# The setup stores, the early weight loads and the relation sums of a graph-network kernel, put in another order

## The chip, the cores and the metric

The kernel runs on one core of one Trainium2 chip. The metric is device microseconds of one execution; several executions are timed and the median is given. A profile comes from one further execution. The engines are named as the profile names them: PE (TensorE, the matmuls; PEld is its weight load), DVE (VectorE), ACT (ScalarE), POOL (GpSimd) and SP (SyncE, which only starts transfers). PSUM is the memory that matmuls write, SBUF the working memory, DRAM the large one. Each engine works through its own instructions in order, and an instruction that starts a DMA is one of them: what stands behind an instruction that waits, waits too.

## The reference

Eight layers follow each other on a node table `x` of 3125 rows and 256 columns, with 50000 edges (`src`, `dst`, sorted by `dst`); each layer takes the layer norm of `x` and adds its result to `x`. The first four, of which the change touches the first, are cut to what matters here:

```
x = x + rel_graph(ln(x))          # rows of src times one of 16 matrices, by edge type, times a weight, summed by dst
x = x + experts(ln(x))            # 8 experts, 2 per node, gelu
x = x + edge_graph(ln(x))         # embedding rows of src, times edge features @ W_dist, summed by dst, then W_comb
x = x + top_half_mlp(ln(x))
...                               # attention graph, experts, max graph, experts
```

```python
transformed = jnp.einsum('ni,rio->rno', h, weight)
msg = transformed[rel_type, src] * norm
out = jax.ops.segment_sum(msg, dst, num_segments=h.shape[0])
```

## The kernel before

**Setup (lines 366 to 679).** The edges come in as [125 x 400] tiles: `dsti` (destinations) on SP's queue, `srci`, `typi`, `wgt` and `norm` on ScalarE's. `x` is loaded in five groups `n_x0` to `n_x4` of five node tiles of 126 rows each (`xs0`, line 415), all on SP's queue. There is a branch for unsorted destinations (line 459), which these inputs do not take. After it the order of PE, DVE, ACT, POOL and SP is the order of the program (`manual_schedule`, line 538): nothing is moved by a scheduler.

The destinations, as floats (`dstf`), are stored to a DRAM table `dsr` (lines 542 and 543), and to the edge records `md` with the sources, the code of destination and type, the weight and a padding (lines 544 to 599). GpSimd gathers from `dsr` the row in which each node's edges begin (`find.fetch`, tile `q_rows`), VectorE counts in it (`find.count`), a small matmul turns the counts into `mixI`, and GpSimd gathers with it the first node tile's edge records (`meta_load`, tile `m_m`). On the same queue of GpSimd, in program order, stand 25 gathers of embedding rows (`species`, tile `n_row`): 5 ahead of the branch, 3 ahead of the two `q_rows` gathers, 7 behind them, and 10 behind `m_m`. VectorE takes the statistics of `x` (`stats`) for groups 0 and 1, then of group 2 woven with the inverse root of the first ten, then norms; groups 3 and 4 come after `mixI`. Each group of five node tiles is stored to the DRAM table `tab` (line 633), 1.26 MB, when its normed rows and its embedding rows are there.

**The tile loop (`stage_one`, line 787 on).** For each of 25 node tiles come 21 windows of 128 edges (17 in the last), and then eight steps of `weigh`. Each of these 29 steps ends in `between()`, one slot. A window gathers 128 rows of `tab` (tile `g`, GpSimd, nine buffers), loads 65 x 128 edge features (tile `f`, SP, six buffers), multiplies `g` with a selection matrix `s` that VectorE has built two windows ahead (`build`, lines 865 and 867; PE line 880 into the PSUM tile `c`), and the features with `w_d` (line 887 into `pw`), which VectorE multiplies with the embedding half of `g` (tile `mt`, line 890). ScalarE copies `c` to `aT` for two windows at once (line 884; `c` has two PSUM banks). `weigh` multiplies `aT` with the 16 relation matrices `w_rel` into one PSUM bank (also called `f` in the profile, line 919), and after its last step VectorE adds this sum to `x` (line 923).

Every second tile a `Flow` begins, for a pair of tiles: `route`, `experts` and `combine`, cut into steps that `between()` hands out slot by slot, so that they fill the engines beside the windows of later tiles. `between()` also advances `bg` (the later search and edge sums), one load of weights (`late_weights`, on ScalarE's queue: `w_rel` in two halves of 2.1 MB in the first two slots, then 0.26 MB pieces of the experts' weights) and one zero store (`first_zeros`, on SP's queue: 32 pieces of 197 KB of the sum table `ex`, then the experts' token tables). After the last tile the Flows that are left run in rounds with nothing beside them.

The rest of the kernel, from 1865 us on, is not touched.

Of the kernel before, what the change touches and what calls it, by code (L numbers as in the profile page):

```python
# [9 lines left out]
F32 = mybir.dt.float32  # L10
# [11 lines left out]
NT = 25  # L22
# [23 lines left out]
TN = 126  # L46
# [49 lines left out]
def tile_gnn_ffn(ctx: ExitStack, tc: tile.TileContext, a: dict, out: bass.AP):  # L96
    nc = tc.nc
# [14 lines left out]
    def ps(tag, shape):  # L112
        return banks["pool"].tile(shape, F32, name=tag, tag=tag, bufs=banks["bufs"][tag])
# [60 lines left out]
    def flat(v):  # L174
        return v.rearrange("(p t) -> p t", p=EP)
# [131 lines left out]
    dsr = dram.tile([EP + 1, ET], F32, name="dsr")  # L307
# [10 lines left out]
    def split(pool, dsti, pre):  # L318

        hii = pool.tile([EP, ET], I32, name=pre + "hii")  # L320
        hif = pool.tile([EP, ET], F32, name=pre + "hif")
        lof = pool.tile([EP, ET], F32, name=pre + "lof")
        dstf = pool.tile([EP, ET], F32, name=pre + "dstf")
        nc.vector.tensor_scalar(hii, dsti, 7, None, op0=OP.arith_shift_right)
        nc.vector.tensor_copy(hif, hii)
        nc.vector.tensor_copy(dstf, dsti)
        nc.vector.scalar_tensor_tensor(lof, hif, -128.0, dstf, op0=OP.mult, op1=OP.add)
        return hif, lof, dstf
# [68 lines left out]
    def rows126(table, t, n):  # L397
        return table[t * TN : (t + n) * TN, :].rearrange("(t p) d -> p t d", p=TN)

    def edge_in(name, dt):  # L400
        t = pp.tile([EP, ET], dt, name="e_" + name)
        nc.scalar.dma_start(t, flat(a[name]))
        return t
# [1 line left out]
    srci = edge_in("src", I32)  # L405
    typi = edge_in("edge_type_16", I32)
    xs0 = []
    for i in range(5):
        xg = pp.tile([P, 5, D], F32, name=f"n_x{i}")
        t = 5 * i  # L410
        m = 5 if i < 4 else 4
        if i == 4:
            nc.gpsimd.memset(xg[:, 4, :], 0.0)
            nc.sync.dma_start(xg[:TV, 4, :], a["x"][(NT - 1) * TN :, :])
        nc.sync.dma_start(xg[:TN, :m], a["x"][t * TN : (t + m) * TN, :].rearrange("(t p) d -> p t d", p=TN))
        xs0.append(xg)
        if i == 0:
            wgt = edge_in("edge_weight", F32)
            norm = edge_in("edge_weight1", F32)
    nc.scalar.dma_start(wd[0:1, :], a["L1_gnn_b_dist"])  # L420
    nc.scalar.dma_start(wd[1:65, :], a["L1_gnn_W_dist"])
    eid = pp.tile([EP, ET], F32, name="e_eid")
# [1 line left out]
    none = pp.tile([1, ET], F32, name="e_none")  # L424
# [34 lines left out]
    with tc.If(uns > 0):  # L459

        rec = dram.tile([E, RW], F32, name="rec")
        with tc.tile_pool(name="srt", bufs=1) as ep, tc.tile_pool(name="srt2", bufs=2) as eb, \
# [13 lines left out]
            hif, lof, dstf = split(ep, dsti, "s_")  # L476
# [11 lines left out]
            for b in range(ET // BT):  # L488
# [11 lines left out]
                for i in range(BT):  # L500
                    j = b * BT + i
# [37 lines left out]

    dstf = pp.tile([EP, ET], F32, name="e_dstf")  # L540
    nc.vector.tensor_copy(dstf, dsti)
    nc.sync.dma_start(dsr[1:, :], dstf)
    nc.sync.dma_start(dsr[:1, :], none)
    nc.sync.dma_start(flat(md[F_DST, :E]), dstf)
    pf = ps("tp", [P, EP])
    nc.tensor.transpose(pf, dstf[:, 0:1].to_broadcast([EP, P]), ident[:EP, :EP])
# [50 lines left out]
    nc.sync.dma_start(flat(md[F_NORM, :E]), norm)  # L597
    nc.sync.dma_start(flat(md2[F_EID - 5, :E]), eid)
    nc.sync.dma_start(md[:, E:].rearrange("f (p c) -> p f c", c=P), pads)


    lt = pp.tile([EP, ET], F32, name="e_lt")
# [46 lines left out]
    def meta_load(t, pool):  # L649
        m = pool.tile([R1, P], F32, name="m_m", bufs=2)  # L650
        gather(m, words(md), mixI[:R1, t : t + 1])
        return m
# [29 lines left out]
    def late_weights(pool, w):  # L682

        def loads(name, dst, src):
            w[name] = dst
            nc.scalar.dma_start(dst, src)

        def rows(m, name):
            k, n = m.shape
            return pool.tile([P, k // P, n], F32, name="w_" + name), m.rearrange("(k p) n -> p k n", p=P)  # L690

        def same(src, n):
            return bass.AP(tensor=src.tensor, offset=src.offset, ap=[[0, P], [1, n]])

        for k in range(2):
            nc.scalar.dma_start(wrel[:, k], a["L0_gnn_weight"][:, k * P : (k + 1) * P, :].rearrange("r p o -> p r o"))
            yield
        loads("rw0", *rows(a["L0_ffn_router_w"], "rw0"))
        loads("b01", pool.tile([P, 16], F32, name="w_b01"), a["L0_ffn_b1"])
        loads("b02", pool.tile([8, D], F32, name="w_b02"), a["L0_ffn_b2"])  # L700
        yield
        w["01"] = pool.tile([P, 8, 2, 256], F32, name="w_01")
        w["02"] = pool.tile([P, 8, 2, 256], F32, name="w_02")
        for e in range(8):
            nc.scalar.dma_start(w["01"][:, e], a["L0_ffn_w1"][e].rearrange("(k p) f -> p k f", p=P))
            yield
            nc.scalar.dma_start(w["02"][:, e], a["L0_ffn_w2"][e].rearrange("(f p) d -> p f d", p=P))
            yield
        loads("c", *rows(a["L1_gnn_W_comb"], "c"))
        yield  # L710
        nc.scalar.dma_start(wfa[:, :, :D], a["L2_gnn_W_func"].rearrange("(k p) n -> p k n", p=P))
        loads("bc", pool.tile([P, D], F32, name="w_bc"), same(a["L1_gnn_b_comb"], D))
        loads("wr", pool.tile([P, D], F32, name="w_wr"), same(a["L1_ffn_wr"], D))
        yield

    def first_zeros():
        exv = ex.rearrange("(p r) d -> p (r d)", p=TN)
        for c in range(0, NT * 2 * D, ET):
            nc.sync.dma_start(exv[:, c : c + ET], zero[:TN])
            yield  # L720
        nc.sync.dma_start(tab2[NX:, :], zero[: NP - NX, :ZW])
        nc.sync.dma_start(rec2[E:, :], zero[:, :2])
        for f in range(3):
            nc.sync.dma_start(md2[f, E:].rearrange("(p c) -> p c", c=P), zero[:NPAD, :P])
        yield
        for x, y in zip(xg2 + xg3, yg2 + yg3):
            w = y.shape[0] // P * D
            v = x[: y.shape[0], :].rearrange("(p r) d -> p (r d)", p=P)
            for c in range(0, w, ET):
                nc.sync.dma_start(v[:, c : min(w, c + ET)], zero[:, : min(w, c + ET) - c])  # L730
                yield
# [55 lines left out]
    def stage_one(late, cp, eb):  # L787
# [83 lines left out]
        cur = {}  # L871
# [42 lines left out]
        def weigh(t, i):  # L914
            if i == 0:
                cur["f"] = ps("f0", [P, D])
            for r in (2 * i, 2 * i + 1):
                for h in range(2):
                    nc.tensor.matmul(cur["f"][:TN], aT[:, h, r, :], wrel[:, h, r, :], start=(r == 0 and h == 0),  # L919
                                     stop=(r == 15 and h == 1))  # L920
            if i == 7:
                x = x_of[t // 2][:TN, t % 2, :]
                nc.vector.tensor_add(x, x, cur["f"][:TN])


        x_of, e_of = {}, {}

        def size(q):
            return min(2, NT - 2 * q)
# [10 lines left out]
        def load_e(q, i):  # L940
            n = size(q)
            e = e_of[q, i] = eb.tile([P, 2, D], F32, name=f"e{i}", bufs=1)
            nc.sync.dma_start(e[:TN, :n], rows126(ex, 2 * q, n)[:, :, i * D : (i + 1) * D])
# [190 lines left out]
        flows = []  # L1134
        bg = background(eb, bank)
        loads, zeros_ = late_weights(late, w), first_zeros()
        slot = 0

        def between(fast=False):
            nonlocal slot  # L1140
            for i, f in enumerate(flows):
                f.step(slot, flows[:i], fast)
            while flows and flows[0].part == 3:
                flows.pop(0)
            if slot < 2 * PERIOD or slot % BG_EVERY == 0:
                next(bg, None)
            next(loads, None)
            next(zeros_, None)
            slot += 1

        meta(0)
# [7 lines left out]
        for t in range(NT):  # L1159
            n = GL if t == NT - 1 else GC  # L1160
            for j in range(n):
                build()
                window(k)
                k += 1

                if j >= 2:
                    at = wins[k - 2][1]
                    if at in (3, 0):
                        add_up(t, 0 if at == 3 else 1)
                if j == 3 and t + 1 < NT:  # L1170
                    raw[t + 1] = meta_load(t + 1, wb)
                if j == META_AT and t + 1 < NT:
                    meta(t + 1)
                if j == 14 and t % 2 == 0:
                    load_x(t // 2)
                if j == 18 and t == 1:
                    beyond(eb, bank())
                if t % 2 and j == 19:
                    load_e(t // 2, 0)
                between()  # L1180
            for i in range(8):
                weigh(t, i)
                if i == 1:
                    add_up(t, 2)
                if i == 7 and (t % 2 or t == NT - 1):
                    if t == NT - 1:
                        load_e(t // 2, 0)
                    flows.append(Flow(t // 2))
                between()
        while flows:  # L1190
            between(True)
# [1349 lines left out]
```

## Time and profile before

| | |
|---|---|
| Median of 3 runs | 4229.56 us (4227.59 to 4244.47) |
| The profiled execution's own time, and its span | 4229.5 us, 4227.7 us |
| Setup: last `tab` store landed | 84.5 us |
| First `f` matmul of `weigh` in the first tile | 148.7 us |
| Last add of a relation sum | 1762.7 us |
| First load of the next stage | 1865 us |
| Busy over the span: PE, DVE, POOL, ACT | 64%, 46%, 42%, 20% |

Section 2 of the profile page cuts the span into 40 slices of 106 us. The digits are tenths of busy time, PEclk the granted clock in tenths:

```
PE   1688999989889999948411365365670112137875
DVE  3445666665665555442344333444662233245300
POOL 4342333341253333002466544544437666643323
DMA  7766455452243444113233254365523333323543
```

The first slice is the setup and the start of the first tile; the tile loop is slices 2 to 17. A share of busy time says little in itself: the waits and the timeline of a stretch say what ended each stretch of idleness. A wait is written `who <- for whom`, with the time in all, the number of times, and the longest.

### The profile page before, as it was taken

The numbers are of one execution on the slowest core, as the hardware profiler recorded it, in microseconds if no ns is written. First come the engines' busy times: TensorE is split into PE (matmuls) and PEld (weight loads), VectorE is DVE, ScalarE is ACT, GpSimd is POOL, SyncE is SP. The second block draws the span as 40 slices with busy tenths as digits, with TensorE's granted clock in tenths as the row PEclk, the third lists the DMA queues.
The fourth block names the chain that finished last, engine by engine and source line by source line (L and its number), as shares of the span: only waits on it lengthen the run. The fifth ranks groups of instructions, "written<-read, shape, count | busy, mean of one in ns | idle before, by whom it ended". The sixth has DMA issues, their size and how long they took to land. (4 is left out here: it accounts for less than half of the span.)

```text
span 4227.7 us, 46661 instructions
## 1 busy us (share of the span) xinstructions
PE 2697.7 (64%) x12940; PEld 2134.4 (50%) x12940; DVE 1946.6 (46%) x7501; ACT 845.3 (20%) x1803; POOL 1758.5 (42%) x1996
## 2 busy tenths in 40 slices
PE   1688999989889999948411365365670112137875
PEld 0566878767677878737310254254550111125653
DVE  3445666665665555442344333444662233245300
ACT  1112232221122222211100021122220000013322
POOL 4342333341253333002466544544437666643323
PEclk9878999999799999968755576577775555566987
DMA  7766455452243444113233254365523333323543
GB/s 223 223 190 187 129 157 144 130 154 65 76 118 107 118 133 126 52 48 107 73 93 91 86 175 141 107 185 168 174 90 101 87 92 88 92 81 107 158 159 100
DMA packets 275971, 521.46 MB, mean 123 GB/s; under 512 B 53609, under 2 KB 176897, under 8 KB 275685
## 3 DMA queue, kind: packets, MB, share of 16 engines
q0 software_dynamic: 105344, 306.57, 25.0%
q1 hardware_dynamic: 159598, 201.27, 15.6%
q10 hardware_dynamic: 10742, 10.34, 0.8%
q8 instruction: 114, 1.87, 0.2%
q14 instruction: 173, 1.41, 0.1%
HBM read 431.19 MB, written 86.78 MB: 123 GB/s over the span
## 5 line engine op out<-in xcount | busy, mean ns | idle before, releaser
L136 POOL DMA_INDIRECT g<-tab,m_si x521 | 498.0, 956 | 989.9 <-DVE mt L890 526.5
L136 POOL DMA_INDIRECT g_rows<-tab,srcI x413 | 401.9, 973 | 300.4 <-DVE ACC L2273 157.3
L136 POOL DMA_INDIRECT g_row<-tab,srcI x413 | 400.4, 970 | 196.3 <-issue 104.6
L880 PEld LDWEIGHTS c<-s,g 128*128 128x128 f32 x2084 | 345.8, 217 | 166.7 <-issue 83.9
L880 PE MATMUL c<-s,g 128*128 128x96 f32 x2084 | 356.1, 299 | 100.1 <-issue 38.2
L887 PE MATMUL pw<-w_d,f 65*128 65x256 f32 x1042 | 374.4, 445 | 14.2 <-DVE mt L890 11.9
L919 PE MATMUL f<-w_rel,aT 128*126 128x256 f32 x1600 | 372.6, 383 | 0.1
L884 ACT COPY aT<-c 128x384 f32<-128x384 f32 (+1 forms) x323 | 237.1, 737 | 595.7 <-PE c L880 397.5
L1982 PE MATMUL mm<-ro_xt,ro_w 128*128 128x192 f32 (+3 forms) x928 | 255.9, 428 | 122.3 <-ACT ro_h L2063 73.1
L919 PEld LDWEIGHTS f<-w_rel,aT 128*126 128x126 f32 x1600 | 300.2, 190 | 50.5 <-issue 5.3
L1651 PE MATMUL tp<-ident,ACC 128*128 128x128 f32 x50 | 16.1, 424 | 462.5 <-DVE ACC L2395 357.2
L890 DVE TENSOR_TENSOR mt<-pw,g 128x256 f32<-128x256 f32 x521 | 218.7, 420 | 159.0 <-PE pw L887 83.8
L1986 PE MATMUL y<-ro_w,ro_h 128*96 128x256 f32 (+2 forms) x1040 | 263.6, 409 | 33.5 <-ACT ro_h L2063 19.1
L1982 PEld LDWEIGHTS mm<-ro_xt,ro_w 128*128 128x128 f32 x928 | 183.8, 221 | 178.4 <-ACT ro_h L2063 80.5
L1651 PEld LDWEIGHTS tp<-ident,ACC 128*128 128x128 f32 x50 | 7.1, 199 | 470.5 <-issue 441.1
L1986 PEld LDWEIGHTS y<-ro_w,ro_h 128*96 128x96 f32 (+2 forms) x1040 | 190.4, 189 | 86.9 <-ACT ro_h L2063 23.1
L1037 PE MATMUL w<-w,b_h 128*126 128x256 f32 x800 | 218.5, 398 | 11.1 <-ACT xt L950 3.0
L1028 PE MATMUL w<-xt,w 128*128 128x252 f32 (+1 forms) x832 | 221.3, 392 | 6.3 <-issue 3.4
L140 POOL DMA_INDIRECT xg<-XX,ro_pos x100 | 101.6, 1016 | 287.6 <-issue 136.5
L2273 DVE SCALAR_TENSOR_TENSOR ACC<-g_rows,g_e,ACC 128x256 f32<-128x256 f32 x413 | 200.9, 486 | 43.9 <-DVE ACC L2273 19.9
L2395 DVE TENSOR_TENSOR ACC<-ACC,g_row 128x256 f32<-128x256 f32 x413 | 173.2, 424 | 67.1 <-DMA g_row<-tab,srcI 48.0
L2240 PE MATMUL pu<-w_s,a_xt 128*128 128x256 f32 x100 | 45.9, 606 | 231.5 <-DVE ACC L2268 104.8
(580 smaller groups left out, 4791.0 us busy)
## 6 DMA issues: line engine op xcount, KB each, us to landing
ro_w<-in_L_ffn_blocks SPq DMA_DIRECT2D x58, 514.0 KB
ro_w<-in_L_ffn_blocks SPq DMA_DIRECT2D x58, 512.0 KB
f<-in_attr_t SPq DMA_DIRECT2D x521, 32.5 KB
xg<-zero SPq DMA_DIRECT2D x78, 200.0 KB
b_at<-in_edge_attr SPq DMA_DIRECT2D x100, 125.0 KB
tabr<-v SPq DMA_DIRECT2D x12, 758.0 KB
g<-tab,m_si POOLq DMA_INDIRECT x521
g_rows<-in_L_ffn_blocks SPq DMA_DIRECT2D x14, 514.0 KB
```

Source lines behind the costliest of these rows:

```text
L136: return nc.gpsimd.indirect_dma_start(out=dst, out_offset=None, in_=table, in_offset=bass.IndirectOffsetOnAxis(ap=idx, axis=0))
L880: nc.tensor.matmul(pc[:, h, o : o + GW], g[:, h * P : (h + 1) * P], sums[k][0], start=True, stop=True)
L884: nc.scalar.copy(aT[:, :, :, b : b + n * GN].rearrange("p k r n -> p k n r"), pc[:, :, : n * GW].rearrange("p k (n r) -> p k n r", r=16))
L887: nc.tensor.matmul(pw, feats.pop(k), wd, start=True, stop=True)
L890: nc.vector.tensor_tensor(mt[0], pw, rows.pop(k)[:, D:], op=OP.mult)
L919: nc.tensor.matmul(cur["f"][:TN], aT[:, h, r, :], wrel[:, h, r, :], start=(r == 0 and h == 0), stop=(r == 15 and h == 1))
L1028: nc.tensor.matmul(ph, w["01"][:, e, k, i * P : (i + 1) * P], xt[:, k, : n * TN], start=(k == 0), stop=(k == 1))
L1037: nc.tensor.matmul(py, last[:, k, i * TN : (i + 1) * TN], w["02"][:, e - 1, k, :], start=(k == 0), stop=(k == 1))
L1982: nc.tensor.matmul(ph, w[:, o : o + P], xt[:, k, :], start=(k == 0), stop=(k == 1))
L1986: nc.tensor.matmul(py, h[:, i, s], w[:, i * D : (i + 1) * D], start=(i == 0), stop=(i == self.fc - 1))
L2273: stt(u, g[:, r, :D], e[:, r0 + r : r0 + r + 1], u, op0=OP.mult, op1=OP.add)
L2395: nc.vector.tensor_tensor(u, u, rows.pop(r), op=OP.max)
```

## The change

Three places are changed.

1. The stores of `dstf` and of one row of -1 into `dsr` go to ScalarE's queue instead of SP's. The loads of groups 2 to 4 of `x` move on SP's queue from ahead of the branch to behind the stores of the edge records. The memset for the last tile's padding moves with group 4, on GpSimd to behind the seven gathers of embedding rows.
2. In `between()` the weight loads begin in slot 2 and the zero stores in slot 6, instead of both in slot 0.
3. The relation sum of tile t is added to `x` in the second window of tile t + 1 (`weighed`), and the Flow of a pair begins there, two slots later; the last tile's is added at once, as before.

```diff
-    for i in range(5):
+
+    def load_x0(i):
         xg = pp.tile([P, 5, D], F32, name=f"n_x{i}")
...
-        if i == 0:
-            wgt = edge_in("edge_weight", F32)
-            norm = edge_in("edge_weight1", F32)
+
+    load_x0(0)
+    wgt = edge_in("edge_weight", F32)
+    norm = edge_in("edge_weight1", F32)
+    load_x0(1)
...
-    nc.sync.dma_start(dsr[1:, :], dstf)
-    nc.sync.dma_start(dsr[:1, :], none)
+    nc.scalar.dma_start(dsr[1:, :], dstf)
+    nc.scalar.dma_start(dsr[:1, :], none)
...
     nc.sync.dma_start(md[:, E:].rearrange("f (p c) -> p f c", c=P), pads)
+    for i in range(2, 5):
+        load_x0(i)
...
-            if i == 7:
-                x = x_of[t // 2][:TN, t % 2, :]
-                nc.vector.tensor_add(x, x, cur["f"][:TN])
+
+        def weighed(t):
+            x = x_of[t // 2][:TN, t % 2, :]
+            nc.vector.tensor_add(x, x, cur["f"][:TN])
+            if t % 2 or t == NT - 1:
+                flows.append(Flow(t // 2))
...
-            next(loads, None)
-            next(zeros_, None)
+            if slot >= 2:
+                next(loads, None)
+            if slot >= 6:
+                next(zeros_, None)
             slot += 1
...
                 window(k)
                 k += 1
+                if j == 1 and t:
+                    weighed(t - 1)
...
-                if i == 7 and (t % 2 or t == NT - 1):
-                    if t == NT - 1:
-                        load_e(t // 2, 0)
-                    flows.append(Flow(t // 2))
+                if i == 7 and t == NT - 1:
+                    load_e(t // 2, 0)
+                    weighed(t)
```

## The prediction

> **What bounds the kernel now.** I read the slices of the page first, then the waits and the timeline of the first 150 us, then TensorE's waits in the long tile loop. The chain that ended last starts only at 3997 us, so it says nothing of the place that the change touches; I followed that chain by hand.
>
> The waits of GpSimd and VectorE up to 90 us (who waited <- for what: us in all, times, longest):
>
> ```profile
> POOL q_rows L136 <- DMA dsr<-e_dstf: 16.3, 1, 16.3
> ...
> DVE j L798 <- DMA tab<-n_row: 24.4, 1, 24.4
> DVE q_rows L578 <- DMA q_rows<-dsr,q_rowi: 13.0, 2, 12.5
> ```
>
> The reader is to see a stall in the setup: GpSimd does nothing for 16.3 us until the destinations are in DRAM (`dsr`), and VectorE ends the setup with 24.4 us of waiting for `tab`. The timeline shows why (start, us, engine, line, what, count):
>
> ```profile
> 19.45 6.80 SPq L415 DMA_DIRECT2D n_x<-in_x  x1
> 35.23 0.32 SPq L542 DMA_DIRECT2D dsr<-e_dstf  x1
> ...
> 19.57 0.37 DVE L541 CAST e_dstf<-dsti 125x400 f32<-125x400 int32 x1 [6.92 <-DVEq L459]
> ...
> 39.76 0.91 POOL L136 DMA_INDIRECT q_rows<-dsr,q_rowi  x1 [16.33 <-DMA dsr<-e_dstf]
> ...
> 52.21 0.97 POOL L136 DMA_INDIRECT m_m<-md,mixI  x1 [1.21 <-DVE n_st L616]
> ...
> 65.29 1.00 POOL L136 DMA_INDIRECT n_row<-in_L_gnn_embed_table,l_z  x1 [0.30 <-issue]
> ```
>
> `e_dstf` is ready at 19.94, its store leaves SP at 35.23: it stands behind x's loads, each of which waits for the DMA eight before it to land (eight completion semaphores in turn, by the built program). Behind it GpSimd's 17 remaining embedding gathers (1.30 us apart) end at 66.3, the last `tab` store can only then go, and `tab` is complete at 84.5. Nothing of the tile loop starts before. The windows of 5 us show what the DMA engines do (columns: busy us of PE, PEld, DVE, ACT, POOL; clock; DMA share; GB/s):
>
> ```profile
> 30.00:35.00 5.00, 0.00 (x0) 0.00 (x0) 4.36 (x25) 0.50 (x1) 0.00 (x0) 1.00 0.11 32
> 35.00:40.00 5.00, 0.00 (x0) 0.00 (x0) 0.00 (x0) 4.52 (x10) 0.24 (x1) 1.00 0.26 78
> ...
> 70.00:75.00 5.00, 0.00 (x0) 0.00 (x0) 0.00 (x0) 0.00 (x0) 0.00 (x0) 1.00 0.93 350
> ```
>
> They idle during the stall and are full afterwards, to about 150 us (0.93 at 300 GB/s on average over 90 to 148.7). So the first tile, too, is held by transfers. From 407 to 1762 us TensorE is busy 1270 of 1355 us; what it waits for is small:
>
> ```profile
> PE c L880 <- issue: 20.9, 18, 5.3
> PE c L880 <- DVE s L865: 15.6, 13, 3.8
> PE pw L887 <- DVE mt L890: 7.9, 9, 1.4
> ```
>
> **What the Trainium skill says.** "DMA: Bandwidth & Descriptors", Issuing engines are not separate DMA queues: a DMA issued on another engine saves only the issuer's time. The trace agrees as to issue (0.32 us for the store) but here 15 us of waiting stood ahead of it in SP's order, and that is what the move takes away; it brings no bandwidth. Same page, Measured: 1 MB moves at 341 GB/s, 16 MB at 425; the trace's best slice of the setup is 375, so I price a full queue at 350. "TensorE: Matmul & The Clock Gate", What's actually happening: the array runs at half clock until it has been busy for about 3.4 us. The trace has it: four `c` matmuls take 1.01 us at 93.9 and 0.58 at 146.67, though the granted clock reads 1.00 in both; a first tile with fewer gaps may warm sooner. I take nothing for that.
>
> **Part 1: destinations on ScalarE's queue, x2 to x4 behind.** Removed: the wait of 15.3 us (35.23 - 19.94). ScalarE has nothing until its activation at 24.24; the two stores (0.32, 0.21) and the table load (1.28) behind them end by 22, so that costs nothing. From issue to GpSimd's gather took 4.5 us (39.76 - 35.23): the gather can go at 24.5. The two `q_rows` gathers (1.22 apart) and seven embedding gathers (1.30) end at 36.1. Without the cover of that work the gain on GpSimd would be the whole 15.3; but the next gather, `m_m`, needs VectorE's count.
> VectorE: statistics of groups 0 and 1 end at 29.6 as now; group 2 is loaded late. SP issues `srcf` at about 22.6 and is through `pads` 4.4 us later (as 36.25 to 40.66 now), x2 goes at 27.0. It is 0.63 MB behind about 0.8 MB of md stores; at 220 GB/s (what 5 to 20 us show) that lands at about 33. VectorE so stalls 3.5 us, and the norms of groups 0 and 1 move from 34.3 to 38. Then the counts, already landed, follow at once: `mixI` at 41.5 instead of 49.7, `m_m` (2.5 us later, as now) at 44 instead of 52.2, say 9 us earlier with rounding. x4's load waits on SP for a memset that now sits behind the seven gathers on GpSimd (36.4); it lands by about 42 and is used at about 45, so it is hidden; should x3 or x4 be 5 us late, the norms of the last 15 tiles are (50 to 55), still ahead of GpSimd's end. GpSimd's last gather ends at 57.3 (66.3 - 9). The cut stores and two `tab` stores stand behind x4's load on SP, and go at 41 to 44, as now (43.03).
> From GpSimd's end to `tab` complete are 18.2 us now (84.5 - 66.3). In that stretch the first half of `w_rel`, 2.1 MB issued at 58.24, shares the engines: 6 us at 350 GB/s. Part 2 takes it out. `tab` complete: 57.3 + 18.2 - 6 = 69.5, that is 15 us earlier.
>
> **Part 2: weights from slot 2, zeros from slot 6.** The 2.1 MB now load inside the first tile, whose transfers fill the engines: +6 us (7 at the 300 GB/s of that stretch; bound below by 0 if it fits between gathers, above by the 15.6 us that ScalarE stood at 94 to 110, when its in-order queue waited at the DMAs behind the other half and `aT`, the evacuation of `c`, with them). Six zero pieces of 0.197 MB leave the first tile: -4 us at 300 GB/s. They come after slot 115, where the DMA share is 0.62 (250 to 407): hidden, at most +4. The embedding `e` of the first pair is read at slot 48, the last `ex` zero goes at slot 37: no new wait.
>
> **Part 3: the sum added in the next tile.** The same 25 adds of 0.42 us. VectorE waits 133.2 us in 22 of them, 6 each, but TensorE is at work then. Without it VectorE does the last slot's steps and the next selection matrices before the tile ends instead of after: at 463.57 it adds, and the first `s` comes 1.6 us later, while TensorE shows no gap at all. What can be had lies in the 15.6 and 7.9 us quoted; I take a fifth, -5 us over the loop (bounds: 0 and -20, nearly all). Each Flow starts two slots later; the PSUM bank of the sum is free 20 slots before it is needed. At the end Flow 11 is two rounds behind: about 98 rounds from 1763 to 1864, so 1.03 each, +2 us.
>
> **Sum.** -15 + 6 - 4 - 5 + 2 = -16, against the profiled execution's own 4229.5 us (span 4227.7 and 1.8 around it), which is within 0.1 us of the median of the three runs. So 4214.
>
> **Rivals.** *More* (4200): nothing of `w_rel` is paid (it loads while gathers wait on GpSimd's 1.25 us each), and every boundary gives 0.6 us: -15 - 4 - 13 + 2 = -30. For it: first-tile gaps of 4 to 6 us that are latency, not bytes. Against: the DMA share is 1.0 in half of the slices there. *Given back* (4224): the first tile is bound by its bytes. Setup gives 15, `w_rel` behind ScalarE's queue takes 12 instead of 6, the boundaries nothing, the tail 2: with the -4 of the zeros -5. For it: `aT` stood 15.6 us behind one such load. *Slower* (4254): the two slots put the Flows' VectorE-heavy steps (norms, top 2, adds from PSUM) against windows where VectorE has no slack. VectorE is busy 810 of 1355 us, 2 of 3 in windows, and TensorE lost 24 us to it; if each of 24 boundaries then costs TensorE 1.5 us more, +36, and with -11 from the rest and no gain +25. It decides above 1.3 us a boundary (32 us). Against: waiting there falls by 6 us each, and the steps are the same. That the change does not do what it says is excluded: the built program has the stores on ScalarE's queue and x2 to x4 behind `pads`.
>
> **How the numbers follow.** Likeliest 0.45 (4214, own range 4204 to 4223); more 0.25; given back 0.20; slower 0.10. 0.5%, 21 us, is about what a measurement of this kernel can tell from no change (three runs lay 17 us apart): below 4208 lie most of "more" and a fifth of the likeliest, 0.34; above 4251 0.08; between them 0.58. The range of 8 in 10 runs from 4196, the low end of "more" (all of the boundary waits), to 4232 ("given back" with the upper bound for `w_rel`); "slower" stays outside.
>
> **What would show it.** Right: `dsr` from ScalarE at about 20, the first `q_rows` gather at 24 to 26, `m_m` at 43 to 45, `tab` complete (the first `f` loads) at 67 to 72, the first `f` matmul at 134 to 140 instead of 148.7; VectorE's waits for the sum near zero and TensorE's waits on `s` and `mt` smaller. Wrong: `m_m` still at 50 (x2 late), `tab` after 78, a ScalarE gap over 20 us at slots 3 to 6, or a stretch from the first to the last `f` matmul (1613 us now) that has grown.

## The result: 0.3% slower

| | before | after |
|---|---|---|
| Median | 4235.8 us | 4250.1 us |
| Ratio of the times | 1 | 1.003, 95% interval 1.0019 to 1.0042 |
| Span of the profiled execution | 4227.7 us | 4245.8 us |
| Last `tab` store landed (first `f` load) | 84.6 us | 77.4 us |
| First `f` matmul | 148.7 us | 142.0 us |
| From there to the last `f` matmul's end | 1613.9 us | 1628.6 us |
| From there to the next stage's first load | 102.35 us | 102.94 us |

The change wins 6.7 us ahead of the first relation sum, half of what I forecast, and loses 14.7 us in the tile loop, where I had forecast a small gain. The next stage so begins 8.6 us late. The other 9.5 us between the two spans come after it; the stretch from the last `f` matmul to the end lay between 2452 and 2479 us in the profiles on these chips, whatever the edit, so a single pair of profiles says nothing there.

**The setup.** The waits of VectorE and GpSimd up to 90 us, after (us in all, times, longest):

```profile
DVE j L803 <- DMA tab<-n_row: 20.3, 1, 20.3
...
POOL m_m L136 <- DVE n_mv L623: 10.6, 1, 10.6
DVE n_st L621 <- DMA n_x<-in_x: 10.2, 1, 10.2
...
POOL q_rows L136 <- DVE rs_v L199: 5.8, 1, 5.8
```

GpSimd's wait of 16.3 us for `dsr` has become one of 5.8. Two waits of over 10 us stand in its place: VectorE for the third group of `x`, and GpSimd ahead of `m_m`. The timeline, after:

```profile
23.81 0.52 ACTq L545 DMA_DIRECT2D dsr<-e_dstf  x1
...
28.99 3.19 SPq L416 DMA_DIRECT2D n_x<-in_x  x2
...
29.47 0.92 POOL L136 DMA_INDIRECT q_rows<-dsr,q_rowi  x1 [5.77 <-DVE rs_v L199]
...
39.47 0.43 DVE L621 BATCH_NORM_STATS2 n_st<-n_x 126x6 f32<-126x256 f32 x1 [10.18 <-DMA n_x<-in_x]
...
51.71 0.98 POOL L136 DMA_INDIRECT m_m<-md,mixI  x1 [10.63 <-DVE n_mv L623]
...
64.75 1.00 POOL L136 DMA_INDIRECT n_row<-in_L_gnn_embed_table,l_z  x1 [0.30 <-issue]
```

The first `q_rows` gather is 10.3 us earlier than before, and `m_m` only 0.5 us: everything won on GpSimd is waited away at 41.1 to 51.7. The windows show that the DMA engines now work during what was a stall (0.11 of their time at 32 GB/s from 30 to 35 us before) and are full later as before:

```profile
30.00:35.00 5.00, 0.00 (x0) 0.00 (x0) 0.00 (x0) 0.00 (x0) 3.78 (x5) 1.00 0.69 214
...
70.00:75.00 5.00, 0.00 (x0) 0.00 (x0) 0.00 (x0) 0.00 (x0) 0.00 (x0) 1.00 0.89 319
```

What is gained of `tab` comes from its last stretch: from GpSimd's end to the last store landed are 11.6 us (65.75 to 77.4) instead of 18.2. That `w_rel` no longer stands beside it is a part of this and not the whole: with part 2 alone (below) the stretch is 14.9 us, with part 1 alone 16.5.

**The loop.** TensorE's waits from 400 to 1762 us, after:

```profile
PE pw L892 <- DVE mt L895: 16.4, 11, 3.1
PE w L957 <- ACT b_h L1038: 12.1, 7, 2.9
PE c L885 <- issue: 11.9, 16, 1.6
PE w L957 <- ACT xt L958: 11.4, 5, 6.3
PE c L885 <- DVE s L870: 9.7, 12, 1.7
```

Of the waits that I meant to win back, those at `c` have shrunk (`issue` and `s` from 36.5 us to 21.6), and that at `mt` has grown (7.9 to 16.4). New are the second and fourth line: line 957 is the transpose in `flip_rows`, and it waits 23.5 us for ScalarE. Before, the same transpose (there line 949) has one such wait:

```profile
PE w L949 <- ACT xt L950: 1.9, 1, 1.9
```

One place of the seven, on TensorE, after:

```profile
657.98 1.12 PE L1036 MATMUL w<-xt,w 128*128 128x252 f32 x4
...
659.82 0.26 PE L809 MATMUL w<-ident,m_m 105*128 105x105 f32 x1
661.49 0.43 PE L957 MATMUL w<-ident,xn 126*128 126x126 f32 x2 [1.42 <-ACT b_h L1038]
```

and the same stretch before:

```profile
656.54 1.05 PE L1028 MATMUL w<-xt,w 128*128 128x252 f32 x2
...
658.84 0.38 PE L949 MATMUL w<-ident,xn 126*128 126x126 f32 x2
...
663.10 0.26 PE L804 MATMUL w<-ident,m_m 105*128 105x105 f32 x1
```

All three write PSUM tiles called `w`, and `w` has two banks (`psums(c0=2, pw=2, agg=1, f0=1, w=2)`), taken in turn. Before, the Flow's first transpose of `xn` took the bank beside that of an expert's matmul, and the transpose of the next tile's edge records (`meta`, tile `m_m`) came two windows later. Two slots later the Flow's step falls into the same slot as `meta`, right behind it: `m_m` takes the second bank, and `xn` must wait until ScalarE's gelu has read the first. In the order of the program a Flow's transpose stands right behind `m_m`'s in 9 of 25 tiles before and in 21 of 25 after. The number of such neighbours is not the price by itself: in the nine places of before a transpose of `xn` stands ahead of `m_m`'s and one of `v` follows 0.1 us behind it, with no wait to speak of. In after the matmul ahead is an expert's in 10 of the 21 places, and the transpose behind begins up to 6.6 us after `m_m`'s.

### The profile page after: what moved, and what is told of

Read it like the earlier page. It is cut to its first block, busy times and chain, and to the rows that moved or that the text cites. A ratio compares the mean times of both kernels' runs of the same rounds, so it can differ in the third digit from the quotient of the medians.

```text
span 4245.8 us, 46630 instructions
## 1 busy us (share of the span) xinstructions
PE 2686.5 (63%) x12940; PEld 2128.5 (50%) x12940; DVE 1948.8 (46%) x7501; ACT 844.5 (20%) x1803; POOL 1763.1 (42%) x1996
## 5 line engine op out<-in xcount | busy, mean ns | idle before, releaser
L924 PEld LDWEIGHTS f<-w_rel,aT 128*126 128x126 f32 x1600 | 302.1, 191 | 57.3 <-issue 8.2
L1662 PE MATMUL tp<-ident,ACC 128*128 128x128 f32 x50 | 16.3, 428 | 462.5 <-DVE ACC L2406 462.5
L1997 PEld LDWEIGHTS y<-ro_w,ro_h 128*96 128x96 f32 (+2 forms) x1040 | 189.6, 188 | 84.4 <-issue 23.8
L1047 DVE SCALAR_TENSOR_TENSOR x<-w,b_comb,x 126x256 f32<-126x256 f32 x200 | 96.1, 480 | 230.3 <-PE w L1045 213.0
```

Of the source, the lines that this page charges most:

```text
L1997: nc.tensor.matmul(py, h[:, i, s], w[:, i * D : (i + 1) * D], start=(i == 0), stop=(i == self.fc - 1))
```

## The experiments

All ratios are against the kernel before on the same chip. The six last runs fell on chips where that kernel takes 3761 to 3762 us, the others on chips where it takes 4230 to 4236 us; ratios are compared, not times.

### The three parts one by one

`e1_setup` is part 1 alone, `e2_slots` part 2, `e3_sum` part 3, each with the lines of the diff shown above. `e4_flow_late` leaves the add at the tile's end and only begins each Flow two slots later:

```diff
-                if i == 7 and (t % 2 or t == NT - 1):
-                    if t == NT - 1:
-                        load_e(t // 2, 0)
-                    flows.append(Flow(t // 2))
+                if i == 7 and t == NT - 1:
+                    load_e(t // 2, 0)
+                    flows.append(Flow(t // 2))
...
                 k += 1
+                if j == 1 and t and t % 2 == 0:
+                    flows.append(Flow(t // 2 - 1))
```

> Part 1 alone (destinations on ScalarE's queue, x2 to x4 behind the edge records). Theory: it gains nothing, because x2 now lands late and VectorE, which needs x2's statistics before the norms and the counts, is late at m_m: m_m at 51 to 52, GpSimd's last embedding gather at 64.5 to 65.5, tab complete (first f load) at 83 to 85, first f matmul 147 to 149, loop from first to last f matmul 1614 +- 3, time within 3 us of before. Rival (setup is worth what I predicted, the other parts took it): m_m at 44, tab complete at 75, time 8 us or more below before.

> Part 2 alone (weights from slot 2, zeros from slot 6). Theory: it is the whole gain at the start: tab complete at 77 to 79 (the half of w_rel no longer shares the engines with the tab stores), first f matmul at 141 to 143, loop 1614 +- 3, so 5 to 8 us faster than before. Rival (later zeros and weights slow the tiles behind): the loop grows by 8 us or more, and the time is the same as before or slower.

> Part 3 alone (relation sum added in the second window of the next tile, Flows two slots later). Theory: it is the whole loss: first f matmul 148 to 149 as before, loop 1626 to 1636 instead of 1614, time 10 to 22 us above before. Rival (parts 1 and 2 cost the loop): loop 1614 +- 3 and the time within 4 us of before.

> Kernel before with the add where it was, and only the Flows beginning two slots later. Theory phase (two slots later, the Flows' transposes and VectorE steps fall on windows where TensorE waits for them): the loop grows as in part 3 alone, 1626 to 1636. Theory place (VectorE's add in window 1, which waits for the end of the tile's f matmuls and holds back the multiplications of window 1, is the loss): the loop stays at 1614 +- 3 and the time within 4 us of before.

| | ratio, 95% interval | first `f` load | first `f` matmul | loop |
|---|---|---|---|---|
| part 1 | 0.9990 (0.9976 to 1.0005) | 82.4 | 147.8 | 1611.3 |
| part 2 | 0.9995 (0.9981 to 1.0010) | 81.0 | 145.1 | 1603.2 |
| part 3 | 1.0034 (1.0019 to 1.0049) | 87.1 | 153.0 | 1634.9 |
| Flows late only | 1.0034 (1.0023 to 1.0046) | 83.2 | 148.3 | 1606.6 |

Part 3 is the whole loss, and the Flows' two slots alone lose as much, with every add where it was. Parts 1 and 2 are each within what can be measured of nothing. The loop column is one profiled execution: the late Flows' was the fastest of its 22 runs (4222.9 us, median 4243.9), and one execution says little of a few us: the loops of the kernel before, of parts 1 and 2 and of the kernels below that are not slower lie between 1603 and 1620 us on these chips. So my forecast of 1626 to 1636 us for it missed, while the times bear it out. Part 2 alone was to bring `tab` to 77 to 79 us and the time down by 5 to 8; it did neither, so that the 7 us at the start come only from parts 1 and 2 together. How far one profile scatters there can be read from the last two rows, whose setup is that of before: 87.1 and 83.2 us. In the six profiles with the setup and the slots of after, the first `f` load is at 75.3 to 79.1 us.

### What in two slots costs so much

Four kernels, on one chip. `e5_sum_phase` is part 3 with each Flow's schedule counted from two slots back; `e6_meta8` is the kernel before with only `meta` two slots earlier; `e7_meta11` is the kernel after with `meta` one slot later; `e8_flow4` is `e4_flow_late` with four slots.

```diff
# e5, on part 3 alone
-                    self.gen, self.since, self.done = make(self.q), slot, 0
+                    self.gen, self.since, self.done = make(self.q), slot - (0 if self.part or fast else 2), 0
# e6, on the kernel before
-META_AT = 10
+META_AT = 8
# e7, on the kernel after
-META_AT = 10
+META_AT = 11
# e8, on e4_flow_late
-                if j == 1 and t and t % 2 == 0:
+                if j == 3 and t and t % 2 == 0:
```

> Part 3 alone, but each Flow's schedule counted from two slots back, so that from its second slot on it stands where it stood before; only the add itself is late. Theory phase: the loss of part 3 (0.34%) is gone, time within 0.1% of before (4227 to 4235 where before is 4231), waits of TensorE on ScalarE ahead of the Flows' transposes back under 5 us. Theory place (the add in window 1 costs): 0.2% or more above before.

> Kernel before, Flows untouched, but the transpose of the next tile's edge records (m_m, slot of window 10) made two slots earlier, in window 8's. Theory collision (two slots later, the Flow's first transposes of xn land in the same slot right behind the transpose of m_m; both write w, which has two PSUM banks, so the second needs the bank that a gelu on ScalarE still reads): the loss appears without the Flows being moved, 0.2 to 0.4% above before, and TensorE waits 15 to 25 us on ScalarE ahead of the xn transposes (2.5 before). Theory load (the Flows' steps as such lie badly against the windows and the f matmuls): no change, within 0.1%.

> Kernel after, with the transpose of m_m one slot later (window 11), which parts it from the Flow's transposes again. Theory collision: most of the loss goes, from 0.3% above before to within 0.1% of it or below (its early gain of 7 us is there), and TensorE's waits on ScalarE ahead of the xn transposes fall from 24 us to under 6. Theory load: it stays 0.3% above.

> Kernel before with the Flows four slots late instead of two (the add where it was). Theory collision: at four slots the xn transposes are behind window 12's slot and clear of m_m's, so the loss is smaller than at two slots: 0 to 0.15% above before. Theory load (every slot later is worse): 0.34% or more, about 0.7%.

| | Flow's transpose behind `m_m`'s, of 25 | TensorE on ScalarE ahead of the Flows' transposes, us | ratio, 95% interval |
|---|---|---|---|
| after | 21 | 23.8 | 1.0030 (1.0019 to 1.0042) |
| `e5_sum_phase` | 9 | 2.5 | 1.0017 (1.0001 to 1.0033) |
| `e6_meta8` | 21 | 13.8 | 1.0063 (1.0037 to 1.0089) |
| `e7_meta11` | 1 | 2.7 | 1.0000 (0.9984 to 1.0015) |
| `e8_flow4` | 0 | 6.0 | 0.9993 (0.9979 to 1.0008) |

The kernel before, with no Flow and no add moved, is made 0.63% slower by one constant that brings `meta` into the Flow's slot, and the kernel after is brought back by moving `meta` out of it. Four slots late cost nothing: the load theory, for which later is worse, is out. `e6_meta8` loses more than I expected; beside the transposes, the experts' matmuls, which write `w` too, wait there:

```profile
PE w L1028 <- ACT xt L950: 14.6, 8, 2.7
...
PE w L949 <- ACT b_h L1030: 10.6, 5, 3.6
```

`e5_sum_phase` shows what became of VectorE's wait for the relation sum. Before, it stood at the add for the most part (from 400 to 1762 us):

```profile
DVE x L923 <- PE f L919: 126.8, 20, 9.9
...
DVE mt L890 <- PE pw L887: 58.9, 59, 2.7
```

With the add late, VectorE's waits in the same stretch read:

```profile
DVE mt L890 <- PE pw L887: 174.2, 73, 10.6
```

It waits at the next instruction that needs TensorE: 115 us more there. It won nothing, and the ratio even suggests a small cost of the late add. Part 3 and the late Flows alone, on one chip, do not show such a cost: both are at 1.0034.

### The bank, or the engines in that slot; and the setup

`e9_meta_bank` changes nothing in the order of the kernel after; `m_m`'s transpose only writes the bank of the relation sum, which is free from window 1 to `weigh`:

```diff
-            pt = bank()[:, 0, :R1]
+            pt = ps("f0", [P, D])[:, :R1]
```

`e10_setup_fix` is parts 1 and 2 with `x2` still loaded ahead of the branch, and the memset of `n_x4` at the start of GpSimd's program. `e11_best` is that with the bank edit, `e12_best_flow4` has the Flows four slots late as well.

```diff
+    xlast = pp.tile([P, 5, D], F32, name="n_x4")
+    nc.gpsimd.memset(xlast[:, 4, :], 0.0)
...
     load_x0(1)
+    load_x0(2)
...
-    for i in range(2, 5):
+    for i in range(3, 5):
         load_x0(i)
```

> Kernel after, with nothing moved, but the transpose of m_m writes the PSUM bank of the relation sum (free between the add in window 1 and the f matmuls) instead of one of the two banks of w. Theory bank (the Flow's first xn transpose must wait for the bank that a gelu still reads, because m_m's transpose took the other): most of the loss goes as with m_m one slot later, 0.0 to 0.1% above before, TensorE's waits on ScalarE ahead of the xn transposes under 8 us (23.5 in after). Theory engines (VectorE's six small steps on m_m and ScalarE's norm in one slot are the clash, not the bank): 0.25 to 0.35% above before.

> Kernel before with parts 1 and 2, but x2 still loaded ahead of the branch and the padding memset at the start of GpSimd's program, so that VectorE need not wait for x2 and x4's load not for GpSimd. Theory (x2's late landing ate what the early destinations gave): no VectorE wait on x2, m_m at 43 to 45 instead of 52, last embedding gather at 57 to 58, tab complete (first f load) at 67 to 71, first f matmul at 131 to 137, and 8 to 16 us below before (0.2 to 0.4%). Rival (what is won in the setup is given back in the first tiles, whose transfers fill the engines): first f matmul at 140 or later or the loop longer by as much, time within 0.15% of before.

> The same setup as the run above and part 2, no part 3, and m_m's transpose in the bank of the relation sum. If the collision costs something in the kernel before too (9 of its 25 m_m transposes have a Flow's transpose right behind), it is 2 to 6 us below the run above; otherwise within 3 us of it. 8 to 20 us below before in all.

> The run above with the Flows four slots late. With m_m in a bank of its own the phase of the Flows should no longer matter: within 0.1% of the run above. Theory load: 0.2% or more slower than it.

| | ratio, 95% interval | `mixI` | `m_m` | first `f` load |
|---|---|---|---|---|
| `e9_meta_bank` | 0.9977 (0.9966 to 0.9989) | | 52.4 | 78.1 |
| `e10_setup_fix` | 0.9973 (0.9961 to 0.9985) | 43.1 | 52.7 | 77.4 |
| `e11_best` | 0.9966 (0.9953 to 0.9980) | | 52.2 | 76.8 |
| `e12_best_flow4` | 0.9974 (0.9962 to 0.9986) | | | |

It is the bank. With the same instructions in the same order, and VectorE's and ScalarE's work in that slot untouched, the kernel after goes from 0.30% above before to 0.23% below it, and TensorE no longer waits on ScalarE ahead of any Flow's transpose (8.6 us in 4 places are left ahead of the experts' first matmuls). Which of the two banks of `w` every later user gets shifts with the edit as well; that is the same effect. The edit wins back 0.53%, more than the 0.34% that part 3 had lost; 0.17% is to be had in the kernel before too (`e14_before_bank`, below), and what is left of the gain, 0.36%, is about the loss of part 3. With it, the Flows' place makes no difference that shows: the last two rows' intervals overlap.

`e10_setup_fix` gains what I gave, 0.27%, but not by the way I gave: `m_m` and the first `f` load are where they were in after. That the gain is the fix's isn't shown either: parts 1 and 2 without it are worth about 0.2% where both kernels have the bank edit (`e15_no_sum_bank` against `e14_before_bank`, on one chip: 3747.0 and 3753.5 us). `x2` is no longer waited for (one wait of 3.7 us is left, for `x4`), the counts are ready at 43.1 us, and `m_m` still goes at 52.7. The timeline of `e10_setup_fix`:

```profile
34.18 0.43 DVE L671 TENSOR_SCALAR e_lt<-e_cu,srt 125x400 f32<-125x400 f32 x1
...
34.40 5.59 SPq L417 DMA_DIRECT2D n_x<-in_x  x1
40.09 2.43 SPq L672 DMA_DIRECT2D md<-e_lt  x1
...
43.10 0.22 DVE L654 TENSOR_SCALAR mixI<-tp,q_off 105x2 int32<-105x2 f32 x1 [0.67 <-issue]
...
52.74 0.97 POOL L136 DMA_INDIRECT m_m<-md,mixI  x1 [9.25 <-DVE n_st L623]
```

`m_m` reads `md`, and the last row written there is the cut weight `lt`. It is ready at 34.6, but its store stands on SP behind `x4`'s load, whose issue lasts from 34.4 to 40.0; the issue of the store itself ends at 42.5, and the gather goes 10 us later. The releaser that the profile infers for `m_m`, a statistic on VectorE, isn't one: in the trace an instruction of GpSimd's queue ahead of the gather waits from 40.3 to 51.9 us for the completion semaphores of two stores to `md`, and the later store is that of `lt`.

### The store of the cut weights, and what is left

`e13_cut_first` moves `x3` and `x4` behind the two cut stores; `e14_before_bank` is the kernel before with the bank edit alone; `e15_no_sum_bank` the kernel after with it and without part 3; `e16_cut_bank` is `e13_cut_first` with the bank edit.

```diff
# e13, on e10_setup_fix
-    for i in range(3, 5):
-        load_x0(i)
...
     nc.sync.dma_start(flat(md2[F_W1 - 5, :E]), cu)
+    for i in range(3, 5):
+        load_x0(i)
```

> The kernel with x2 ahead of the branch, with x3 and x4 now loaded behind the two stores of the cut weights (lt and cu) instead of ahead of them. Theory store (GpSimd's m_m gather reads md and so waits for the store of lt, which stood behind x4's load on SP until 42.5 us and landed at 52; the counts in mixI were ready at 43.1): m_m at 42 to 46, last embedding gather at 55 to 59, tab complete (first f load) at 67 to 72, 12 to 20 us below before (0.3 to 0.5%). Rival (m_m is held by something else, or the bytes of the setup fill the engines anyway): m_m still at 51 to 53, or tab complete at 75 or later, and 8 to 11 us below before as without this edit.

> Kernel before with m_m's transpose in the bank of the relation sum and nothing else. If the two banks of w cost something in the kernel before too, 0.1 to 0.2% below before; if only the two-slot shift made the collision, within 0.05% of it.

> Kernel after without part 3 (the sum added at the tile's end, Flows where they were), m_m's transpose in the bank of the relation sum. The kernel after with that bank was 0.23% below before. Theory (part 3 costs nothing but the collision): within 0.1% of that. Rival (the late add costs VectorE or TensorE in itself): 0.35 to 0.45% below before.

> x2 early, x3 and x4 behind the cut stores, part 2, no part 3, m_m's transpose in the bank of the relation sum: 0.05 to 0.1% below the first run of this group, 0.4 to 0.6% below before if both gains add up.

The last pair, on one chip, tells the late add from the Flows' place: `e17_sum_bank` is `e9_meta_bank` once more, `e18_add_back` the same with the add at the tile's end and the Flows begun in window 1 as in `e4_flow_late`.

> Kernel after with m_m's transpose in the bank of the relation sum, once more, as the companion on the same chip of the run below: 0.15 to 0.3% below before.

> The same kernel with the add back at the tile's end and only the Flows two slots late. Theory add (the late add holds VectorE at the start of the next tile, ahead of mt, and costs something in itself): 0.1 to 0.25% below its companion. Theory phase (what is left of part 3's price is the place of the Flows): within 0.07% of it.

| | ratio, 95% interval |
|---|---|
| `e13_cut_first` | 0.9969 (0.9957 to 0.9980) |
| `e14_before_bank` | 0.9983 (0.9976 to 0.9990) |
| `e15_no_sum_bank` | 0.9959 (0.9944 to 0.9974) |
| `e16_cut_bank` | 0.9952 (0.9934 to 0.9969) |
| `e17_sum_bank` | 0.9968 (0.9955 to 0.9981) |
| `e18_add_back` | 0.9948 (0.9931 to 0.9965) |

The store was it. GpSimd in `e13_cut_first`:

```profile
42.55 1.00 POOL L136 DMA_INDIRECT n_row<-in_L_gnn_embed_table,l_z  x1 [0.31 <-issue]
43.86 0.97 POOL L136 DMA_INDIRECT m_m<-md,mixI  x1 [0.30 <-issue]
```

`m_m` now follows the gather ahead of it without a wait, and GpSimd's last gather ends at 57.9. But the first `f` load stays at 77.0, because another wait has grown, VectorE's for `x3` and `x4`:

```profile
DVE n_st L621 <- DMA n_x<-in_x: 11.8, 2, 5.9
```

The norms of the last 15 tiles begin after 59.5 us, and the last three `tab` stores leave SP only at 63.8 to 66.7. That `m_m` is early is worth nothing as long as `x` and the cut weights stand behind each other on SP; both orders were tried, and both end at 77.

The bank edit gains 0.17% in the kernel before as well; which waits it takes away there isn't shown. `e18_add_back` is 0.2% below its companion, and five of its six runs are faster than all nine of the companion's; the intervals of `e15_no_sum_bank` and `e18_add_back` overlap, and `e5_sum_phase` was 0.17% above before. So the late add costs something like 0.2% once the bank is free, and the Flows' place nothing that shows. With the bank taken the add's cost does not show (`e3_sum` and `e4_flow_late`, both 1.0034). TensorE's listed waits from 400 to 1762 us are the same in both (63 and 65 us); where the add's cost lies isn't shown.

`e16_cut_bank` and `e18_add_back` beat both kernels, by 0.48% and 0.52% against before; between them nothing can be told.

## Why the prediction was wrong

**Part 3, the failed step.** "Each Flow starts two slots later; the PSUM bank of the sum is free 20 slots before it is needed." I followed the bank of the sum and not the two banks of `w`, which the moved steps themselves use, and priced the two slots at nothing in the loop. They cost 0.34% (`e4_flow_late`), 14 us; what they do in the kernel after is 23.8 us of waiting ahead of the Flows' transposes for a bank that ScalarE still reads, 1.9 us before. What I should have done was to list what else the program issues in the slot where the Flow's steps now land; the order of the program shows it without a run. The gain of 5 us at the boundaries failed as well: "what can be had lies in the 15.6 and 7.9 us". Those waits did shrink in part, but VectorE's wait only moved from the add to `mt`, and with the bank free the late add costs about 0.2%.

The rival *Slower* named the Flows' steps against the windows, and that is where it happened, but for another resource: VectorE's lack of slack. It is answered by `e9_meta_bank`, which leaves VectorE's work as it is. Its price, 1.5 us a boundary, was too high: 14.7 us over 24 boundaries are 0.6. I discarded it with "the steps are the same", which is true of the steps and not of their neighbours. The Trainium skill, "Perfetto Trace Analysis", Matmuls, says that independent matmul groups should rotate through different PSUM banks so that an evacuation overlaps the next group; the traces agree, and put a price on one more user of two banks in the same slot: 23.8 us of waits against 1.9.

**Part 1.** The chain was right as far as the first gather, and each link late:

| | predicted | after |
|---|---|---|
| `dsr` leaves ScalarE | 20 | 23.8 |
| first `q_rows` gather | 24.5 | 29.5 |
| `x2` landed; VectorE's stall | 33; 3.5 | 39.4; 10.2 |
| counts in `mixI` | 41.5 | 46.4 |
| `m_m` | 44 | 51.7 |
| GpSimd's last gather ends | 57.3 | 65.8 |
| `tab` complete | 69.5 | 77.4 |

The failed step is "the next gather, `m_m`, needs VectorE's count". It also needs the rows that it reads: the cut weights' store, issued at 44.25 in after. I had read that store as "as now" and not followed who waits for it. The 2.5 us that lay between counts and gather before, and that I carried along as fixed, were the rest of that store's wait: it left at 41.2, the counts came at 49.7, GpSimd's queue waited for the store's semaphore until 51.4, and the gather went at 52.2. Two causes that end so close together look like one. My price for `x2`'s lateness was a third of the real one, and `e10_setup_fix` shows that without it nothing would have moved either. The step from 8.2 us (52.2 - 44) to "9 us earlier" was a rounding too far, of 0.8 us.

The reading of the 15.3 us was incomplete as well. In the kernel before, SP has issued the last load of `x` at 26.3; after that it stands at the end of the branch, where it waits for the eight completion semaphores, one after the other, until the loads issued ahead of the branch have landed. ScalarE's store needs one of these eight semaphores, and SP has to be through with it first, so the move to ScalarE's queue did not take it out of this wait: `e_dstf` is ready at 19.56 in after, SP is through with that semaphore at 23.7, and the store leaves at 23.81. With `x2` ahead of the branch again (`e10_setup_fix`) it leaves at 25.9. SP's waits at the branch (ns of one, least/median/most, then the first and the last start in us), before and after:

```profile
L459 SPq EVENT_SEMAPHORE  x8: 17/17/17, 31.7 to 34.8; - x8
...
L462 SPq EVENT_SEMAPHORE  x8: 17/17/17, 22.0 to 23.9; - x8
```

**Part 2 and the rest.** That `w_rel` beside the `tab` stores costs 6 us is not borne out: the stretch behind GpSimd's end became 6.6 us shorter in after (18.2 to 11.6), but with part 2 alone only 3.3 (to 14.9). Inside the first tile it and the six zeros came to 0.5 us net (7.2 us won at `tab`, 6.7 at the first `f` matmul), where I had +6 and -4. The tail was +0.6 for +2. So the sum -15 + 6 - 4 - 5 + 2 came out as -7.2 + 0.5 + 14.7 + 0.6 = +8.6. The two speeds of the `c` matmuls are in the trace as the prediction says; the 3.4 us are not: from 114.8 to 124.4 us of before TensorE's timeline has no gap that the profile lists, and four `c` matmuls still take 1.01 to 1.17 us.

## What to carry to other kernels

When a group of steps is moved as a whole, its inner order is the same, but its neighbours are not: list, for the new place, what else takes from the same small pool of PSUM banks, in the order of the program, and which engine still reads the bank that comes next. A wait that ends within a few us of another hides it; before pricing its removal, write down everything that the released instruction reads, with the time at which each was ready. And an instruction freed of a wait on an in-order engine gains only if nothing behind it on that engine waits for something that comes as late as before.

## What was not expected of the hardware

The kernel before took 4230 to 4236 us beside the kernel after and the first twelve runs, and 3761 to 3762 us beside the last six, on other chips. In the profiles the loop differs by 5% (1613.9 us, and 1535.7 with the bank edit), the work behind it by 16% (2465.1 us and 2060.4, where the code is the same). The mean granted clock over the span was 0.78 and 0.81, the mean DMA rate 123 and 139 GB/s for the same bytes; the cause isn't shown.

The gather that reads a store of 195 KB by SP went 7.5 us after the store's issue in after (44.25 to 51.7) and 10 us after it in `e10_setup_fix` (42.5 to 52.7), behind and beside other transfers; for the store of `dsr`, of the same size, it was 5.7 us (23.81 to 29.47).
